# A recurrent decoder layer done by halves of its tokens, with the next layer's key parts on ScalarE

## The chip, the cores and the metric

The kernel runs on one core of a Trainium2 chip. Its metric is the device time of one execution in microseconds (us). Engines are named as the profile names them: PE is TensorE (PEld its weight loads), DVE is VectorE, ACT is ScalarE, POOL is GpSimd, SP is SyncE, whose queue issues nearly all transfers.

## The reference, cut to what matters

Four decoder layers run on 1024 tokens of 128 features; each has a mixing part ("attn"), a cross-attention over a context of 6404 rows ("xattn") and a feed-forward part ("ffn"), each with a layer norm ahead and a residual behind. The change is in the mixing part of layer 2, a gated recurrence with a small MLP. For its input `x` (the layer-normed tokens) it computes, cut to the core:

```python
h = rmsnorm(x, norm1_w)
gate = h @ W_gate.T                      # 192 channels
u = h @ W_in.T
u = causal_conv(u, conv_w) + conv_b      # 4 taps a channel
ig, rg = u @ rg_in_w.T + rg_in_b, u @ rg_gate_w.T + rg_gate_b
alpha = exp(-8 * softplus(forget_lambda) * sigmoid(rg))
xbeta = sqrt(1 - alpha * alpha + 1e-06) * sigmoid(ig) * u
hrec[t] = alpha[t] * hrec[t - 1] + xbeta[t]
x = x + (gelu(gate) * hrec) @ W_out.T
n2 = rmsnorm(x, norm2_w)
return x + (gelu(n2 @ mlp_gate_w.T) * (n2 @ mlp_up_w.T)) @ mlp_down_w.T
```

Behind it, the cross-attention of layer 2 takes queries from the tokens and keys from the context (`k = context @ Wk.T`).

## The kernel before

`build` (L1879) calls the twelve parts in order. Inside a part the statements are handed to a scheduler that sets the order of instructions on each engine and adds the semaphore waits, so an engine's order can differ from the order of the code; each engine takes its instructions strictly in its order. The tokens stay in SBUF as `x` (`x_tok` in the profile), token-major: 128 partitions by 8 tiles of 128 features. `xT` is the normed input with the features on the partitions and 1024 tokens along the row.

`l2_attn` (L1055) is the part that is changed. In order:

- L1079 to L1091 make the constants of `forget_lambda` (`sp`), tiny 96x2 instructions that each need the one before.
- L1094 `normalised` (L291: statistics, a square root on ACT, eight multiplications) writes `xn`; `rmsnormed` (L310) makes `r` from it: one square of 128x1024, one reduction, a square root on ACT, eight multiplications by tiles; `transposed` (L278) turns it into `xT` by PE in two halves of 512 tokens (`BANK` is 512), which DVE evicts with the factor `n1` (L289).
- L1103 to L1108: products of `xT` with `W_gate` (evicted by ACT with Gelu) and `W_in` (evicted by DVE into `up`), by cuts of 96 channels and halves of tokens. PE runs them through `hidden` (L338); the profile calls its line L343.
- L1111 to L1115: the convolution on DVE, per cut one L1112 and three L1114 over all 1024 tokens.
- L1119 to L1125: the two gates (`ig`, `al`), two products each, a sigmoid on ACT, and Exp on `al`.
- L1127 to L1135: `be = sqrt(1 - al*al)`, times `ig` on POOL (L1130), times `u` on DVE, then the scan (one instruction for each cut, along 1024 tokens, L1134) and the product with `gate`, all over 1024 tokens.
- `onto` (L1138) projects to the tokens and adds, both halves in one call; then the second norm and transposition, `x += xn` on POOL (L1153), the MLP (L1155 to L1160) and `onto` again.

Between these, `beside(n)` takes n steps of the generator `split_keys` (L1185), which prepares the next layer's keys: 13 chunks of up to 512 context rows. A chunk is one PE product (L1209), a copy to SBUF on DVE (`k`, L1212), and `split` (L1172): a cast to bf16 on DVE (L1178), the rest on POOL (L1179), a cast of the rest on DVE (L1180), a last subtraction on POOL (L1181), and six transfers of 128 KB by SP (L1183) into `kd2` in DRAM. `k` and `rest` have one buffer, the parts have three. The order of `beside` is 2, 2, 1, 2, 3 chunks; `_run(keys)` takes the last three. Layer 3's keys go through the same generator with a bias `bk`, and its queries and layer 2's through `split`.

`l2_xattn` (L1375) reads the key parts back (`kP`, L1397), makes its queries (L1404), projects the values (L1236) and then runs score products (L1339).

Of the kernel before, what the change touches and what calls it, by code (L numbers as in the profile page):

```python
# [10 lines left out]
F32 = mybir.dt.float32  # L11
# [4 lines left out]
ALU = mybir.AluOpType  # L16
# [195 lines left out]
class Decoder:  # L212
# [62 lines left out]
    def m(self, ps):  # L275
        return ps.tile([P, BANK], F32, tag="m", name="m")

    def transposed(self, ps, dst, src, scale=None):  # L278

        nc = self.nc  # L280
        for h in range(2):
            m = self.m(ps)
            for i in range(4):
                nc.tensor.transpose(m[:, i * P:(i + 1) * P], src[:, 4 * h + i, :], self.ident)  # L284
            o = dst[:, h * BANK:(h + 1) * BANK]
            if scale is None:
                self.copy(o, m)
            else:
                nc.vector.tensor_scalar(o, m, scale, None, ALU.mult)  # L289
# [17 lines left out]
        self.normalised(self.xn, self.x)  # L307
        self.transposed(ps, self.xT, self.xn)

    def rmsnormed(self, out, src, tmp):  # L310

        nc = self.nc
        rs = self.sm.tile([P, NT], F32, tag="rs", name="rms")
        nc.vector.tensor_tensor(tmp, src, src, ALU.mult)
        nc.vector.tensor_reduce(rs, tmp, AX.X, ALU.add)
        nc.scalar.activation(rs, rs, AF.Sqrt, bias=self.eps[:, 0:1], scale=1.0 / D)
        nc.vector.reciprocal(rs, rs)
        for t in range(NT):
            nc.vector.tensor_scalar(out[:, t, :], src[:, t, :], rs[:, t:t + 1], None, ALU.mult)

    def add_bias(self, b):

# [732 lines left out]
    def l2_attn(self):  # L1055
# [6 lines left out]
        with tc.tile_pool(name="h", bufs=1) as pool, tc.tile_pool(name="h_ps", bufs=2, space=PSUM) as ps0:  # L1062
# [7 lines left out]
            def beside(n):  # L1070
                for _ in range(n):
                    next(keys, None)

            def small(name):
                return pool.tile([96, 2], F32, tag=name, name=name)


            y, z, z2, sp = small("sp_y"), small("sp_z"), small("sp_z2"), small("sp")
            nc.vector.scalar_tensor_tensor(y, lam, -1.0, lam, ALU.mult, ALU.min)  # L1079
# [10 lines left out]
            nc.vector.scalar_tensor_tensor(sp, sp, 2.0, y, ALU.mult, ALU.add)  # L1090
            nc.vector.tensor_scalar(sp, sp, -8.0, None, ALU.mult)  # L1091

            beside(2)
            self.normalised(self.xn, self.x)  # L1094
            beside(2)
            tmp = pool.tile([P, NT, D], F32, tag="tmp", name="tmp")
            r = pool.tile([P, NT, D], F32, tag="r", name="r")
            self.rmsnormed(r, self.xn, tmp)
            self.transposed(ps, self.xT, r, n1)
            gate = pool.tile([96, 2, S], F32, tag="gate", name="gate")  # L1100
            up = pool.tile([96, 2, S + 3], F32, tag="up", name="up")
            nc.gpsimd.memset(up[:, :, 0:3], 0.0)
            for c in range(2):  # L1103
                cs = slice(96 * c, 96 * c + 96)
                for h, hs, m in self.hidden(ps, [wgate[:, cs]], [self.xT]):
                    nc.scalar.activation(gate[:, c, hs], m[:96, :], AF.Gelu)
                for h, hs, m in self.hidden(ps, [win[:, cs]], [self.xT]):
                    nc.vector.tensor_copy(up[:, c, 3 + h * BANK:3 + (h + 1) * BANK], m[:96, :])  # L1108
            beside(1)
            u = pool.tile([96, 2, S], F32, tag="u", name="u")  # L1110
            for c in range(2):  # L1111
                nc.vector.tensor_scalar(u[:, c, :], up[:, c, 0:S], cw[:, 4 * c:4 * c + 1], cb[:, c:c + 1], ALU.mult, ALU.add)  # L1112
                for k in range(1, 4):
                    nc.vector.scalar_tensor_tensor(u[:, c, :], up[:, c, k:k + S], cw[:, 4 * c + k:4 * c + k + 1], u[:, c, :],  # L1114
                                                   ALU.mult, ALU.add)  # L1115
            ig = pool.tile([96, 2, S], F32, tag="ig", name="ig")
            al = pool.tile([96, 2, S], F32, tag="al", name="al")
            be = pool.tile([96, 2, S], F32, tag="be", name="be")
            for c in range(2):  # L1119
                for o, wt, bias in ((ig, wri, bi), (al, wrg, bg)):  # L1120
                    for _, hs, m in self.hidden(ps, [wt[:, 192 * i + 96 * c:192 * i + 96 * c + 96] for i in range(2)],
                                                [u[:, i, :] for i in range(2)]):
                        nc.scalar.activation(o[:, c, hs], m[:96, :], AF.Sigmoid, bias=bias[:, c:c + 1])
            for c in range(2):
                nc.scalar.activation(al[:, c, :], al[:, c, :], AF.Exp, scale=sp[:, c:c + 1])  # L1125
            beside(2)
            nc.vector.tensor_tensor(be, al, al, ALU.mult)  # L1127
            nc.vector.tensor_scalar(be, be, -1.0, 1.0, ALU.mult, ALU.add)
            nc.scalar.activation(be, be, AF.Sqrt, bias=self.eps[:96, 1:2])
            nc.gpsimd.tensor_tensor(be, be, ig, ALU.mult)  # L1130
            nc.vector.tensor_tensor(be, be, u, ALU.mult)
            rec = pool.tile([96, 2, S], F32, tag="rec", name="rec")
            for c in range(2):
                nc.vector.tensor_tensor_scan(rec[:, c, :], al[:, c, :], be[:, c, :], 0.0, ALU.mult, ALU.add)  # L1134
            nc.vector.tensor_tensor(rec, rec, gate, ALU.mult)  # L1135
            beside(3)

            def onto(dst, src, wt):  # L1138

                for h in range(2):  # L1140
                    m = self.m(ps)
                    for i in range(4):
                        t = 4 * h + i
                        for c in range(2):
                            nc.tensor.matmul(m[:, i * P:(i + 1) * P], lhsT=src[:, c, t * P:(t + 1) * P],
                                             rhs=wt[:, c * P:(c + 1) * P], start=c == 0, stop=c == 1)
                    d = dst[:, 4 * h:4 * h + 4, :].rearrange("p t d -> p (t d)")
                    nc.vector.tensor_tensor(d, d, m, ALU.add)

            onto(self.xn, rec, wout)  # L1150
            self.rmsnormed(r, self.xn, tmp)
            self.transposed(ps, self.xT, r, n2)
            nc.gpsimd.tensor_tensor(self.x, self.x, self.xn, ALU.add)  # L1153
            _run(keys)
            for c in range(2):  # L1155
                cs = slice(96 * c, 96 * c + 96)
                for _, hs, m in self.hidden(ps, [wmg[:, cs]], [self.xT]):
                    nc.scalar.activation(gate[:, c, hs], m[:96, :], AF.Gelu)
                for _, hs, m in self.hidden(ps, [wmu[:, cs]], [self.xT]):
                    nc.vector.tensor_tensor(gate[:, c, hs], gate[:, c, hs], m[:96, :], ALU.mult)  # L1160
            onto(self.x, gate, wdown)

# [4 lines left out]

    KPART, QPART = (0, 1, 2, 0, 1, 0), (0, 0, 0, 1, 1, 2)  # L1170

    def split(self, pool, src, dst, which, a, b):  # L1172

        nc = self.nc
        n = b - a
        p = [pool.tile([P, BANK], BF16, tag=f"part{i}", name=f"part{i}", bufs=3) for i in range(3)]
        rest = pool.tile([P, BANK], F32, tag="rest", name="rest")
        nc.vector.tensor_copy(p[0][:, :n], src)  # L1178
        nc.gpsimd.tensor_tensor(rest[:, :n], src, p[0][:, :n], ALU.subtract)  # L1179
        nc.vector.tensor_copy(p[1][:, :n], rest[:, :n])  # L1180
        nc.gpsimd.tensor_tensor(p[2][:, :n], rest[:, :n], p[1][:, :n], ALU.subtract)  # L1181
        for i, k in enumerate(which):
            nc.sync.dma_start(out=dst[:, i, a:b], in_=p[k][:, :n])  # L1183

    def split_keys(self, ps, pool, w, kd, bk=None, mask=None):  # L1185
# [19 lines left out]
        for c in range((NK + BANK - 1) // BANK):  # L1205
            a, b = c * BANK, min((c + 1) * BANK, NK)
            n = b - a
            m = self.m(ps)
            nc.tensor.matmul(m[:, :n], lhsT=w, rhs=self.ctxT[:, a:b], start=True, stop=True)  # L1209
            k = pool.tile([P, BANK], F32, tag="k", name="k")  # L1210
            if bk is None:
                nc.vector.tensor_copy(k[:, :n], m[:, :n])  # L1212
            else:
                nc.vector.tensor_scalar(k[:, :n], m[:, :n], bk, None, ALU.add)
            self.split(pool, k[:, :n], kd, self.KPART, a, b)
            yield
            if mask is not None:
                row = pool.tile([1, BANK], F32, tag="row", name="row", bufs=1)
                self.mask_row(row[:, :n], rows, 4 * c, n)
                m = self.m(ps)  # L1220
                nc.tensor.matmul(m[:, :n], lhsT=first, rhs=row[:, :n], start=True, stop=True)  # L1221
                bar = pool.tile([P, BANK], BF16, tag="bar", name="bar")
                nc.vector.tensor_copy(bar[:, :n], m[:, :n])
                nc.sync.dma_start(out=kd[:, 6, a:b], in_=bar[:, :n])
                nc.sync.dma_start(out=kd[:, 7, a:b], in_=three[:, :n])
                yield
# [679 lines left out]
```

## Time and profile before

| what | us |
|---|---|
| median of 3 runs shown | 6175.1 |
| lowest and highest of them | 6174.22, 6192.93 |
| the profiled execution's own time | 6182.17 |
| its span | 6180.4 |
| from the last addition of layer 1 (3620.4) to the last addition of `l2_attn` (3732.8) | 112.4 |

Mean granted TensorE clock over the span: 0.944. A time such as 3620.4 is counted from the span's start. The table of stretches of time gives the busy time of every engine in each stretch with the number of instructions in brackets, then the granted clock as a share of full speed and the transfer engines' share. A timeline has start, length, engine, line, operation, output and inputs, shapes, count, and in square brackets how long the engine had been idle and whose result ended it. The mean length of an instruction holds the time in which it was held up after its start.

### The profile page before, as it was taken

Reading aid. Unit: us, or ns where it says so; the run is one execution under the profiler, and the core shown is the slowest. Engines: PE = TensorE matmul, PEld = TensorE weight load, DVE = VectorE, ACT = ScalarE, POOL = GpSimd, SP = SyncE. Lnnn points to the kernel's source line nnn. Section 1 sums busy time; section 2 is a strip of 40 time slices with the busy share of each in tenths; the row PEclk is TensorE's granted clock in tenths of the full one; section 3 lists DMA queues with packets and bytes.
Section 4 is the critical chain, followed back from the end, with each engine's and each line's share of the span. In section 5 each row is a group of like instructions: output and inputs, shape, how many; then the busy total and the mean of one; then the engine's idle time right before and its main releaser. Section 6 shows DMA issues by size and latency. Waiting matters only on the chain. (4 is left out here: it accounts for less than half of the span.)

```text
span 6180.4 us, 72184 instructions
## 1 busy us (share of the span) xinstructions
PE 5749.6 (93%) x29144; PEld 2078.1 (34%) x29144; DVE 3757.0 (61%) x4571; ACT 3096.5 (50%) x4041; POOL 2254.1 (36%) x1088
## 2 busy tenths in 40 slices
PE   5899999999999999999899968999989689999999
PEld 2333333333333434333476423111124311111126
DVE  6587777777777777776325552100014799999923
ACT  2434444444444444444211225899951167888872
POOL 2057767677777767678321541100001000000000
PEclk7899999999999999999979977999999689999999
DMA  3000000000000000000000013200022100000000
GB/s 113 4 1 1 1 1 1 1 1 1 1 1 1 1 1 1 1 17 18 33 1 14 0 58 87 88 11 7 1 83 80 54 1 22 1 22 1 1 6 29
DMA packets 65200, 117.97 MB, mean 19 GB/s; under 512 B 10475, under 2 KB 46673, under 8 KB 63201
## 3 DMA queue, kind: packets, MB, share of 16 engines
q1 hardware_dynamic: 64288, 110.08, 5.5%
q8 instruction: 228, 3.74, 0.3%
q10 hardware_dynamic: 576, 3.28, 0.1%
q14 instruction: 108, 0.88, 0.0%
HBM read 81.88 MB, written 31.42 MB: 18 GB/s over the span
## 5 line engine op out<-in xcount | busy, mean ns | idle before, releaser
L741 POOL TENSOR_TENSOR tot<-tot,p 128x1024 f32<-128x1024 f32 (+1 forms) x800 | 1889.8, 2362 | 584.5 <-ACT p L732 569.0
L732 ACT ACTIVATE p<-p,drop,keep 128x1024 f32<-128x1024 f32 (+1 forms) x816 | 1011.8, 1240 | 1321.7 <-DVE p L731 1260.0
L669 DVE TENSOR_REDUCE mx<-m 128x2 f32<-128x1024 f32 (+1 forms) x832 | 982.4, 1185 | 496.3 <-PE m L668 479.8
L1275 DVE TENSOR_REDUCE mx<-m 128x2 f32<-128x1024 f32 (+4 forms) x928 | 1027.1, 1159 | 93.5 <-PE m L265 82.2
L731 DVE TENSOR_TENSOR p<-s,every 128x1024 f32<-128x1024 f32 (+1 forms) x816 | 991.5, 1215 | 73.2 <-PE s L726 34.7
L1347 ACT ACTIVATE p<-s 128x512 f32<-128x512 f32 (+4 forms) x1620 | 819.7, 588 | 238.8 <-PE s L265 238.0
L668 PE MATMUL m<-kT,qT 64*128 64x512 f32 (+1 forms) x3328 | 888.6, 606 | 12.3 <-DVE mx L669 11.6
L1344 ACT ACTIVATE p<-s 128x1024 f32<-128x1024 f32 x918 | 843.9, 1185 | 31.5 <-PE s L1339 24.1
L726 PE MATMUL s<-qT,kT 64*128 64x512 f32 (+1 forms) x3264 | 837.7, 596 | 16.6 <-DVE p L731 15.4
L713 PE MATMUL acc<-p,v 128*64 128x512 f32 (+1 forms) x3264 | 809.4, 606 | 4.8 <-ACT p L732 3.8
L1318 PE MATMUL acc<-p,v 128*8 128x512 f32 (+2 forms) x3672 | 621.9, 597 | 0.0
L265 PE MATMUL m<-kP,qP 64*128 64x512 bf16 (+4 forms) x1856 | 371.5, 396 | 102.7 <-DVE mx L1275 57.0
L726 PEld LDWEIGHTS s<-qT,kT 64*128 64x128 f32 (+1 forms) x3264 | 321.7, 185 | 412.5 <-issue 342.1
L668 PEld LDWEIGHTS m<-kT,qT 64*128 64x128 f32 x3328 | 280.7, 185 | 504.1 <-DVE mx L669 371.4
L265 PE MATMUL acc<-p,v 128*9 128x512 f32 (+2 forms) x3240 | 422.2, 593 | 0.0
L265 PE MATMUL s<-qP,kP 64*128 64x512 bf16 (+4 forms) x1620 | 384.0, 387 | 8.9 <-ACT p L1347 6.2
L713 PEld LDWEIGHTS acc<-p,v 128*64 128x64 f32 (+1 forms) x3264 | 198.8, 136 | 550.9 <-issue 457.9
L1339 PE MATMUL s<-qP,kP 48*128 48x512 bf16 (+2 forms) x1836 | 281.0, 384 | 2.7 <-ACT p L1344 1.9
L271 DVE COPY oT<-acc 128x512 f32<-128x512 f32 x14 | 9.7, 690 | 404.4 <-PE acc L1318 395.7
L387 POOL MEMSET mpad<- 128x512 f32 x2 | 1.1, 529 | 641.2 <-PE m L1428 600.4
L265 PEld LDWEIGHTS <-qP 64*128 64x128 bf16 x1856 | 122.7, 96 | 319.6 <-issue 261.9
L265 PEld LDWEIGHTS <-kP 64*128 64x128 bf16 (+1 forms) x1620 | 83.7, 94 | 352.3 <-issue 347.4
(484 smaller groups left out, 4512.5 us busy)
## 6 DMA issues: line engine op xcount, KB each, us to landing
kd<-part SPq DMA_DIRECT2D x156, 128.0 KB, 1.9
wb<-expert_weights SPq DMA_DIRECT2D x30, 512.0 KB, 3.7
kP<-kd SPq DMA_DIRECT2D x24, 512.0 KB, 3.6
kP<-kd SPq DMA_DIRECT2D x48, 192.0 KB, 4.5
w_expert<-in_Y_w SPq DMA_DIRECT2D x8, 768.0 KB, 4.2
qd<-part SPq DMA_DIRECT2D x36, 128.0 KB, 1.8
qP<-qd SPq DMA_DIRECT2D x16, 256.0 KB, 6.2
ctxT<-in_ctxT ACTq DMA_DIRECT2D x4, 800.5 KB, 6.5
```

The source lines that it names most:

```text
L265: return self.tc.keep_in_program_order(self.nc.tensor.matmul(*a, **k))
L668: nc.tensor.matmul(m[:, j, :b - a], lhsT=qT[r, q0:q0 + P], rhs=kT[r, a:b], start=True, stop=True)
L669: tc.keep_in_program_order(nc.vector.tensor_reduce(mx[:, t, :, c:c + 1], m[:, :, :b - a], AX.X, ALU.max))
L713: nc.tensor.matmul(acc[64 * j:64 * j + 64, :], lhsT=v[:n, t, 64 * j:64 * j + 64], rhs=pr[:n, j, :], start=t == 0, stop=t == NKT - 1, tile_ ...
L726: nc.tensor.matmul(s[:n, j, :], lhsT=kT[r, t * P:t * P + n], rhs=qT[r, hs], start=True, stop=True)
L731: tc.keep_in_program_order(nc.vector.tensor_tensor(pr[:n], s[:n], every[:n], ALU.add))
L732: nc.scalar.activation(pr[:n], pr[:n], AF.Exp, bias=drop[:n, t:t + 1], scale=keep[:n, t:t + 1])
L741: nc.gpsimd.tensor_tensor(tot[:n], tot[:n], pr[:n], ALU.add)
L1275: nc.vector.tensor_reduce(mx[:, t, 2 * pair:2 * pair + 2, c:c + 1], m[:, :, :b - a], AX.X, ALU.max)
L1318: matmul(acc[32 * j:32 * j + v.shape[3], off:], lhsT=v[:n, t, 4 * g + j, :], rhs=ws[j][:n, :BANK - off], start=t == 0, stop=t == nkt - 1, ...
L1344: nc.scalar.activation(p2[:n], both[:n], func)
L1347: nc.scalar.activation(pp[j][:n, :w], ss[j][:n, :w], func)
```

## The change

`l2_attn` is rewritten by halves of the tokens; what follows it stands 14 or 15 lines further down.

- `rmsnormed` takes a half `h`: four tiles, its own `rs`. `transposed` takes a list of halves. Each half is normed and transposed by itself.
- The products with `W_in` come ahead of those with `W_gate` and are copied to `up` by ACT.
- The convolution, the gates, Exp, `al*al`, the square root, the products and the scan run on 512 tokens at a time. The scan of the second half starts from the last column of the first (`rec[:, c, BANK - 1:BANK]`). POOL multiplies `ig` with `u` (ahead of the square root) in place of `be` with `ig`.
- The gated result goes to `be`, `onto` does one half a call, and the second norm, the transposition and POOL's `x += xn` follow by halves, as does the MLP.
- The constants of `forget_lambda` stand in the code behind the convolution and the gates.
- Layer 2's key chunks: the copy out of PSUM and both casts go to ACT (`nc.scalar.copy`), where there is no bias; `beside` takes 3, 3, 4 chunks, `_run(keys)` three.

```diff
-    def rmsnormed(self, out, src, tmp):
+    def rmsnormed(self, out, src, tmp, h):
...
+        ts = slice(4 * h, 4 * h + 4)
+        rs = self.sm.tile([P, 4], F32, tag=f"rs{h}", name="rms")
+        nc.vector.tensor_tensor(tmp[:, ts, :], src[:, ts, :], src[:, ts, :], ALU.mult)
...
+            beside(3)
+            self.normalised(self.xn, self.x)
+            beside(3)
...
+            for h in range(2):
+                self.rmsnormed(r, self.xn, tmp, h)
+                self.transposed(ps, self.xT, r, n1, (h,))
...
+            for h, hs in enumerate(halves):
+                for c, cs in enumerate(cuts):
+                    nc.scalar.copy(up[:, c, 3 + h * BANK:3 + (h + 1) * BANK], product([win[:, cs]], [self.xT[:, hs]]))
+            for hs in halves:
+                for c, cs in enumerate(cuts):
+                    nc.scalar.activation(gate[:, c, hs], product([wgate[:, cs]], [self.xT[:, hs]]), AF.Gelu)
...
+            for h, hs in enumerate(halves):
+                for c in range(2):
+                    nc.vector.tensor_scalar(u[:, c, hs], up[:, c, hs], cw[:, 4 * c:4 * c + 1], cb[:, c:c + 1], ALU.mult, ALU.add)
+                    for k in range(1, 4):
+                        nc.vector.scalar_tensor_tensor(u[:, c, hs], up[:, c, k + h * BANK:k + (h + 1) * BANK],
+                                                       cw[:, 4 * c + k:4 * c + k + 1], u[:, c, hs], ALU.mult, ALU.add)
+                for o, wt, bias in ((al, wrg, bg), (ig, wri, bi)):
...
+                        nc.scalar.activation(o[:, c, hs], m, AF.Sigmoid, bias=bias[:, c:c + 1])
+                nc.gpsimd.tensor_tensor(ig[:, :, hs], ig[:, :, hs], u[:, :, hs], ALU.mult)
...
-            nc.scalar.activation(be, be, AF.Sqrt, bias=self.eps[:96, 1:2])
-            nc.gpsimd.tensor_tensor(be, be, ig, ALU.mult)
-            nc.vector.tensor_tensor(be, be, u, ALU.mult)
...
-                nc.vector.tensor_tensor_scan(rec[:, c, :], al[:, c, :], be[:, c, :], 0.0, ALU.mult, ALU.add)
-            nc.vector.tensor_tensor(rec, rec, gate, ALU.mult)
...
+            beside(4)
+            for hs in halves:
+                for c in range(2):
+                    nc.scalar.activation(al[:, c, hs], al[:, c, hs], AF.Exp, scale=sp[:, c:c + 1])
+                nc.vector.tensor_tensor(be[:, :, hs], al[:, :, hs], al[:, :, hs], ALU.mult)
+                nc.vector.tensor_scalar(be[:, :, hs], be[:, :, hs], -1.0, 1.0, ALU.mult, ALU.add)
+            for h, hs in enumerate(halves):
+                nc.scalar.activation(be[:, :, hs], be[:, :, hs], AF.Sqrt, bias=self.eps[:96, 1:2])
+                nc.vector.tensor_tensor(be[:, :, hs], be[:, :, hs], ig[:, :, hs], ALU.mult)
+                for c in range(2):
+                    nc.vector.tensor_tensor_scan(rec[:, c, hs], al[:, c, hs], be[:, c, hs],
+                                                 rec[:, c, BANK - 1:BANK] if h else 0.0, ALU.mult, ALU.add)
+                nc.vector.tensor_tensor(be[:, :, hs], rec[:, :, hs], gate[:, :, hs], ALU.mult)
...
+            for h in range(2):
+                onto(self.xn, be, wout, h)
+                self.rmsnormed(r, self.xn, tmp, h)
+                self.transposed(ps, self.xT, r, n2, (h,))
+                hs = slice(4 * h, 4 * h + 4)
+                nc.gpsimd.tensor_tensor(self.x[:, hs, :], self.x[:, hs, :], self.xn[:, hs, :], ALU.add)
             _run(keys)
...
-    def split(self, pool, src, dst, which, a, b):
+    def split(self, pool, src, dst, which, a, b, cast=None):
+        cast = cast or nc.vector.tensor_copy
...
-        nc.vector.tensor_copy(p[0][:, :n], src)
+        cast(p[0][:, :n], src)
...
-        nc.vector.tensor_copy(p[1][:, :n], rest[:, :n])
+        cast(p[1][:, :n], rest[:, :n])
...
-                nc.vector.tensor_copy(k[:, :n], m[:, :n])
+                nc.scalar.copy(k[:, :n], m[:, :n])
...
-            self.split(pool, k[:, :n], kd, self.KPART, a, b)
+            self.split(pool, k[:, :n], kd, self.KPART, a, b, nc.scalar.copy if bk is None else None)
```

## The prediction

> **What bounds the kernel now.** I read the profile's page first: PE is busy 93% of the span, so a change off PE can pay only where PE stands idle. The edited part is `l2_attn`, found by the lines of its additions: L336 at 3620.4, L1148 last at 3732.1 to 3732.8, hence 112.4 us, 1.8% of the span. The stretches of time, cut where the work changes hands, say who is busy in it:
>
> ```profile
> core 0: us, PE busy (x) PEld busy (x) DVE busy (x) ACT busy (x) POOL busy (x), PEclk, DMA share, GB/s
> 3620.40:3642.40 22.00, 7.08 (x17) 3.29 (x18) 21.63 (x60) 4.66 (x6) 9.58 (x9) 0.69 0.41 137
> 3642.40:3661.60 19.20, 16.28 (x30) 5.50 (x28) 13.68 (x16) 3.65 (x5) 3.71 (x2) 0.82 0.14 48
> 3661.60:3675.00 13.40, 13.16 (x31) 5.07 (x30) 2.23 (x5) 11.41 (x14) 1.79 (x2) 1.00 0.06 20
> 3675.00:3704.00 29.00, 0.00 (x0) 0.00 (x0) 24.10 (x17) 3.27 (x2) 20.82 (x10) 0.58 0.38 127
> ...
> 3732.80:3782.10 49.30, 33.14 (x116) 24.98 (x118) 16.68 (x39) 0.89 (x2) 4.61 (x4) 0.52 0.84 219
> 3782.10:4640.00 857.90, 836.81 (x5155) 171.43 (x5154) 72.67 (x161) 759.17 (x831) 29.97 (x29) 0.98 0.11 35
> ```
>
> The first four I call A, B, C, D; E, F, G are 3704.0 to 3711.7 (projection), to 3718.1 (norm) and to 3732.8 (MLP). In A DVE has no room left (21.63 of 22.00). In D PE does nothing for 29 us and ACT only 3.27: this is DVE and POOL work. DVE's own timeline shows what stands in it:
>
> ```profile
> 3675.72 2.28 DVE L1127 TENSOR_TENSOR be<-al 96x2048 f32<-96x2048 f32 x1
> 3679.04 0.43 DVE L1180 CAST part<-rest 128x512 bf16<-128x512 f32 x1 [1.05 <-POOL rest L1179]
> 3679.38 1.22 DVE L1128 TENSOR_SCALAR be<-be 96x2048 f32<-96x2048 f32 x1
> ...
> 3684.29 0.88 DVE L1178 CAST part<-k 128x512 bf16<-128x512 f32 x1
> 3686.50 4.70 DVE L1180 CAST part<-rest 128x512 bf16<-128x512 f32 x1 [1.33 <-POOL rest L1179]
> 3691.12 0.68 DVE L1212 COPY k<-m 128x512 f32<-128x512 f32 x1
> 3691.83 0.88 DVE L1178 CAST part<-k 128x512 bf16<-128x512 f32 x1
> 3692.63 2.28 DVE L1131 TENSOR_TENSOR be<-be,u 96x2048 f32<-96x2048 f32 x1
> 3695.95 0.43 DVE L1180 CAST part<-rest 128x512 bf16<-128x512 f32 x1 [1.05 <-POOL rest L1179]
> 3696.30 5.37 DVE L1134 TENSOR_TENSOR_SCAN rec<-al,be 96x1024 f32<-96x1024 f32 x2
> ```
>
> A cast of 0.43 takes 4.70 while POOL runs L1130 (4.49 from 3686.42): one waits for the other to end. The recurrence's four DVE steps (L1127, L1131, L1134, L1135) stand in one queue with the key chunks, whose casts wait for POOL. So D is the queue's length, not the recurrence's.
>
> **The change, stretch by stretch.** I laid the changed kernel's instructions out in the order in which its build puts them on each engine, each starting when its inputs are there, with lengths from rows of this profile. Halved shapes: a two-input DVE instruction of 2048 columns takes 2.28, of 1024 1.21 (L314, 128x1024), of 512 0.68 (L1046); L1114 of 1024 takes 1.28, so 0.74 for 512; L1112 0.81, so 0.54; the scan 2.28, so 1.21. On ACT, Exp of 1024 takes 1.15 and the square root of 2048 2.00, which makes 0.72 (512) and 1.15 (1024).
>
> *The key chunks.* DVE loses 13 copies (0.69) and 26 casts (0.43 free, up to 4.70 held up). On ACT the copy costs 0.59 (L273, PSUM to SBUF, 128x512). No row has ACT writing bf16; SBUF to SBUF in f32 ACT takes 0.63 (L439), the only row with bf16 on one side 0.81 (L593, read with two more operands). I take 0.63, the nearest, with 0.43 and 0.81 as ends: the casts have slack nearly everywhere and either end moves the sum by under 2. The second half's scan takes its start from a column; two column operands cost L1112 about 0.12 over L1128's rate, so 0 to 0.2 in all, taken as 0. The Trainium skill's page Perfetto Trace Analysis (Optimizing Scalar/DVE Operations) says that DVE is the faster one where it has a performance mode: the rows agree, 0.43 against 0.63, and were all of the 26 x 0.2 = 5 us on the path, the gain below would be 16. On ACT they stand in a queue that holds little of the recurrence. POOL's two subtractions a chunk (1.15 each) and SP's 78 transfers stay as they are.
>
> *A, 22.0 to 19.0.* Four chunks leave DVE: 4 x 0.60 (a copy's share of the queue) plus eight casts, 3.4, is 5.8. Given back: fixed costs of halves 0.6, the first norm's square root standing in ACT's queue behind a cast that waits for POOL (1.5), POOL in the way of the multiplications (0.7). Ends: gain 0 to 5.8, taken 3.0. The constants of `sp` gain nothing by their place: the scheduler puts them ahead of the norm's multiplications as before. They are 15 steps of 0.19, done 5.0 after the addition, where the norm's square root is ready 4.6 after it.
>
> *B, 19.2 to 13.5.* Before, the convolution starts at 3648.15, 5.75 behind the end of A: PE makes two gate products first and each takes 1.71 at the granted clock of 0.5. Now the products with `W_in` come first and start with the first half of `xT`, 2.9 before the second is there; 1.9 for one product and 0.59 for ACT's copy, and the convolution starts about when A ends. Its own work stays: 4 x (0.54 + 3 x 0.74) = 11.0 plus three POOL subtractions in its way (0.8 each), 13.5, against 13.4 before with the copies in between. Gain 5.7.
>
> *C, 13.4 to 12.5.* PE's 16 gate products (0.86 at full clock) start with the first half of `u`, 4.5 ahead of the end of the convolution, and end 8.6 behind it; then a sigmoid 0.68, a switch of table 1.28, Exp, a key copy and Exp. From the first sigmoid to the square root ACT loads seven tables where it loaded five; the two added (1.28 each) lie beside PE's products. The Trainium skill, page ScalarE: Activation LUTs (What ACT_TABLE_LOAD costs), adds a drain of 1.38 us to every switch, 2.66 in all; that would lengthen the six behind the first sigmoid by 8.3 and leave a gain of 12.7. The trace doesn't show it: a sigmoid ends at 3672.50, the load starts at 3672.52, and Exp 0.01 behind it.
>
> *D, 29.0 to 18.3.* Work left on DVE behind the last Exp: nine two-input instructions of 1.21 or scans of the same length, and one of 0.68: 11.6. POOL still has four chunks here, eight subtractions, and holds up DVE as L1134 shows (scans of 2.28 and 3.17 with POOL at 3.06): seven of them by 0.9 is 6.3, and 0.4 of waits. Ends: none held up, 12.0; all ten behind a whole 1.15, 23.5. What goes is the waiting of DVE's queue for POOL, and POOL's hold-ups are what is late next. The multiplication by `ig` (4.49 on POOL, in the path) is gone from it: POOL does `ig*u` in C. Gain 10.7, between 5.5 and 17.
>
> *E, F, G: 7.7, 5.9, 14.5.* Halves should overlap here, and mostly don't. The first half's 16 projection instructions (3.4 of 6.9) run beside the second scan, but PE's order puts the transposition of the first half ahead of the second half's projection, so that waits for the first half's norm on DVE (3.0): E stays 7.7. F gains 0.5 by the smaller square and reduction. In G, PE has two to three key products and eight MLP products either way (0.86 each, 1.71 before the clock rises); gain 0.2.
>
> Sum: 3.0 + 5.7 + 0.9 + 10.7 + 0 + 0.5 + 0.2 = **21.0 us**, `l2_attn` in 91.4.
>
> *Behind it.* The order on every engine is the same up to `l2_attn` and after it, but for a 1 MB load of weights that SP issues 75 transfers later, hundreds of us ahead of its use in the next part. Up to the first score product 49.3 us go by, set by PE and its one eviction buffer (L1236 and L1240, 13 times 2.86); the key parts read back land 33 us before. So nothing takes the gain back.
>
> Profiled execution: 6182.2 - 21.0 = 6161.2. It stands 7.1 above the median of the runs shown; the median less 21.0 is **6154.1 us**.
>
> **The rivals.**
> - *ACT's queue binds.* ACT now has casts that wait for POOL, ahead of square roots and sigmoids of the path. I have counted three: ahead of the norm's first square root, of Gelu, and of the second half's square root. If five more each cost what a held-up POOL subtraction costs over a free one (3.07 - 1.15 = 1.9), 9.6 go: gain 11.4, 6163.7, within 0.3%. For: POOL is held up in D now. Against: ACT sits idle 25 of D's 29 us.
> - *A switch of table costs twice its load* where it stands between dependent steps: six of 1.28 on the path are 7.7, gain 13.3, 6161.8. Against: the 0.02 above. The drain in the Trainium skill's page ScalarE: Activation LUTs (What ACT_TABLE_LOAD costs) would be such a cost.
> - *ACT's cast is dear, and the kernel slower.* ACT is busy 28.2 in `l2_attn` now. Added: copies 7.7, `up` 2.4, two loads 2.6, halves 1.0, and 26 casts of c. In order, it also waits for POOL's first subtraction once a chunk, 13 x 1.45 = 18.9. That is 60.8 + 26c: level at c = 2.0, and at c = 2.7 it is 131, 18.6 over, 6193.7. For: no row shows this cast. Against: 0.63 and 0.81.
> - *It doesn't do what it says.* True of the constants, as shown; nothing else.
>
> **How the numbers follow.** 0.3% of 6175 is 18.5 us, about what a measurement of this kernel can tell from no change. Forecast 0.82, ACT's queue 0.12, switches 0.02, dear cast 0.04. The forecast's own ends come from A and D: gains of 12.8 and 30.1 with both at one end, of which I take 15 to 28. The gain passes 18.5 in about three quarters of the forecast's share: faster 0.62; the rest of it, the queue and the switches are within 0.3%: 0.34; slower 0.04. Range: 6147 (median less 28) to 6166 (the profiled execution less 16, since the runs shown spread that way, and past both of the middle rivals).
>
> **What would show it.** Right: `l2_attn` at about 91 us; D under 20 us, with DVE free of key lines; the convolution starting within 1 us of the second half of `xT`; an ACT cast near 0.6. Wrong: ACT casts over 1 us; idle times of ACT in D ended by POOL's `rest` with a square root behind them; gaps of over 1 us at table loads; POOL subtractions of 2 to 3 us throughout D; or a longer stretch between the last addition and the first score product, which would mean that the keys' transfers are in the path.

## The result, and the profile after

The changed kernel takes 6159.1 us (median of 7 runs, 6154.84 to 6161.26), the kernel before on the same chip 6177.93 (7 runs): 18.8 us less, ratio 0.9962 with a 95% interval of 0.9951 to 0.9974. The prediction was 6154.1 in 6147 to 6166, faster by over 0.3%. By the ratio the gain is 0.38%; its interval, 0.26% to 0.49%, leaves open whether it is above 0.3%. The profiled execution took 6155.63; its span is 6153.8, 26.6 less than that of before. The last addition of layer 1 now starts at 3618.2 and the last addition of `l2_attn` ends at 3710.8, so the part takes 92.6 where it took 112.4.

The stretches of time of the changed kernel, A to G in the first seven rows, then the way to the first score product and the scores behind it (columns as in the table of before):

```profile
3618.20:3637.90 19.70, 10.81 (x24) 4.59 (x24) 16.89 (x52) 11.62 (x21) 10.33 (x9) 0.78 0.40 134
3637.90:3651.30 13.40, 11.94 (x27) 4.24 (x26) 13.33 (x17) 10.66 (x17) 5.16 (x4) 0.93 0.46 157
3651.30:3663.80 12.50, 12.12 (x29) 4.56 (x27) 1.99 (x3) 12.37 (x17) 4.69 (x2) 1.00 0.00 0
3663.80:3682.50 18.70, 3.75 (x16) 3.48 (x16) 18.21 (x11) 9.64 (x15) 12.97 (x8) 0.58 0.42 144
3682.50:3690.80 8.30, 4.50 (x20) 4.24 (x20) 4.48 (x11) 0.30 (x1) 1.77 (x1) 0.50 0.17 57
3690.80:3696.80 6.00, 3.48 (x8) 1.86 (x9) 3.13 (x9) 1.50 (x3) 1.77 (x1) 0.50 0.01 3
3696.80:3710.80 14.00, 12.68 (x52) 6.82 (x50) 5.24 (x16) 7.96 (x13) 5.97 (x6) 0.97 0.43 142
3710.80:3757.40 46.60, 31.28 (x110) 23.84 (x110) 15.94 (x38) 0.89 (x2) 4.61 (x4) 0.51 0.91 212
3757.40:4615.00 857.60, 837.70 (x5156) 172.43 (x5156) 72.25 (x161) 759.70 (x831) 30.01 (x29) 0.98 0.11 36
```

DVE is down from 21.63 to 16.89 in A, and ACT up from 4.66 to 11.62: the key lines have changed engines. D is 18.7 where it was 29.0, and DVE is still busy through nearly all of it (18.21). DVE's timeline shows with what:

```profile
3663.93 1.22 DVE L1141 TENSOR_TENSOR be<-al 96x1024 f32<-96x1024 f32 x1 [4.33 <-ACT al L1140]
3665.18 1.53 DVE L1142 TENSOR_SCALAR be<-be 96x1024 f32<-96x1024 f32 x1
3666.97 1.22 DVE L1145 TENSOR_TENSOR be<-be,ig 96x1024 f32<-96x1024 f32 x1 [0.26 <-ACT be L1144]
3668.22 4.08 DVE L1147 TENSOR_TENSOR_SCAN rec<-al,be 96x512 f32<-96x512 f32 x2
3672.23 2.11 DVE L1145 TENSOR_TENSOR be<-be,ig 96x1024 f32<-96x1024 f32 x1
3674.26 2.17 DVE L1150 TENSOR_TENSOR be<-rec,gate 96x1024 f32<-96x1024 f32 x1
3676.35 4.19 DVE L1147 TENSOR_TENSOR_SCAN rec<-al,rec,be 96x512 f32<-96x512 f32 x2
3680.58 1.99 DVE L1150 TENSOR_TENSOR be<-rec,gate 96x1024 f32<-96x1024 f32 x1
```

No key line is left, only the recurrence in halves; but a product over 512 tokens that takes 1.22 when free takes 2.0 to 2.2, and a scan 2.06 to 2.17. POOL's subtractions stand beside them. ACT's timeline in the same stretch shows whether its queue binds:

```profile
3667.76 1.15 ACT L1144 ACTIVATE be<-be,eps 96x1024 f32<-96x1024 f32 x1
3668.81 0.60 ACT L1193 CAST part<-k 128x512 bf16<-128x512 f32 x1
3671.26 0.62 ACT L1195 CAST part<-rest 128x512 bf16<-128x512 f32 x1 [1.85 <-POOL rest L1194]
```

ACT waits for POOL here, but behind the last square root, where nothing of the recurrence stands in its queue any more. For the first square root, which stands behind a key cast (0.61) and its table load, DVE waits 0.26 (in the timeline above). The cast takes 0.60 to 0.62.

### The profile page after: what moved, and what is told of

Read it like the earlier page. It is cut to its first block, busy times and chain, and to the rows that moved or that the text cites. A ratio compares the mean times of both kernels' runs of the same rounds, so it can differ in the third digit from the quotient of the medians.

```text
span 6153.8 us, 72228 instructions
## 1 busy us (share of the span) xinstructions
PE 5746.4 (93%) x29144; PEld 2076.6 (34%) x29144; DVE 3740.3 (61%) x4548; ACT 3122.0 (51%) x4091; POOL 2251.7 (37%) x1090
## 5 line engine op out<-in xcount | busy, mean ns | idle before, releaser
L669 PE MATMUL m<-kT,qT 64*128 64x512 f32 (+1 forms) x3328 | 889.5, 607 | 12.5 <-DVE mx L670 11.5
```

What stands on the lines that cost most here:

```text
L669: nc.tensor.matmul(m[:, j, :b - a], lhsT=qT[r, q0:q0 + P], rhs=kT[r, a:b], start=True, stop=True)
```

## The experiments

Three figures are used below: the length of the part (from the last addition of layer 1 to the last of `l2_attn`), the time from the same start to the first score product, and to the 401st exponential of the scores on ACT, some 440 us behind the part. For before they are 112.4, 161.6 and 556.1, for the changed kernel 92.6, 139.2 and 534.4.

**Which half of the change does it: e1, the key lines back on DVE.**

```diff
-                nc.scalar.copy(k[:, :n], m[:, :n])
+                nc.vector.tensor_copy(k[:, :n], m[:, :n])
...
-            self.split(pool, k[:, :n], kd, self.KPART, a, b, nc.scalar.copy if bk is None else None)
+            self.split(pool, k[:, :n], kd, self.KPART, a, b, None)
```

> The halves stay, the key copies and casts go back to DVE. The part took 112.4 us before and 92.6 after. If the gain is wholly DVE's queue being free of key work, it goes back to about 112. If it is wholly the halves, it stays near 92.6. My theory is that both count and add up: DVE has 13 copies and 26 casts more, part of them held up by POOL, in the stretches of the norm and of the scan, so about 101.5, and the median between those of the two kernels.

6169.94 (median of 10 runs; before 6179.11), ratio 0.9984 [0.9974, 0.9993]. Part 102.5, first score product 149.0. Its stretches A and D:

```profile
3615.00:3641.70 26.70, 10.41 (x24) 4.62 (x24) 26.22 (x66) 4.25 (x7) 14.09 (x13) 0.70 0.50 167
...
3665.40:3687.80 22.40, 3.75 (x16) 3.49 (x16) 18.91 (x21) 3.65 (x4) 12.61 (x8) 0.60 0.42 141
```

With the halves alone A is longer than before (26.7 against 22.0), because six chunks now stand there in place of four and DVE has no room (26.22 of 26.70); B is shorter still (10.4): no chunk is left for it, and POOL does nothing there.

**The other half: e2, the kernel before with the key lines on ACT.**

```diff
-                nc.vector.tensor_copy(k[:, :n], m[:, :n])
+                nc.scalar.copy(k[:, :n], m[:, :n])
...
-        nc.vector.tensor_copy(p[0][:, :n], src)
+        cast(p[0][:, :n], src)
...
-        nc.vector.tensor_copy(p[1][:, :n], rest[:, :n])
+        cast(p[1][:, :n], rest[:, :n])
```

> The kernel before, with the key copies and casts on ACT and nothing else changed. By DVE's queue alone the part falls to about 92; by the halves alone it stays at 112. My theory: about 105, since 4.5 us of POOL's product with ig and whole-length steps one behind another stay in the path; the multiplication on POOL then stands ahead of or behind key subtractions as before.

6172.82 (median of 10 runs), ratio 0.9991 [0.9981, 1.0]. Part 105.8, first score product 154.5. A falls by 4.0, to 18.0, but D only by 1.2, to 27.8, though no key line is left on DVE there. DVE's timeline of D is complete in five lines:

```profile
3671.17 2.29 DVE L1127 TENSOR_TENSOR be<-al 96x2048 f32<-96x2048 f32 x1 [13.88 <-ACT al L1125]
3673.49 2.06 DVE L1128 TENSOR_SCALAR be<-be 96x2048 f32<-96x2048 f32 x1
3686.36 3.22 DVE L1131 TENSOR_TENSOR be<-be,u 96x2048 f32<-96x2048 f32 x1 [10.81 <-POOL be L1130]
3689.62 6.22 DVE L1134 TENSOR_TENSOR_SCAN rec<-al,be 96x1024 f32<-96x1024 f32 x2
3695.87 3.06 DVE L1135 TENSOR_TENSOR rec<-rec,gate 96x2048 f32<-96x2048 f32 x1
```

DVE stands idle for 10.81 and waits for the product with `ig` on POOL. ACT's timeline shows the other thing in the way: its square root, whose input is there at 3675.5, stands behind a cast that waits for POOL.

```profile
3677.82 0.62 ACT L1180 CAST part<-rest 128x512 bf16<-128x512 f32 x1 [1.57 <-POOL rest L1179]
3678.46 1.28 ACT L1129 ACT_TABLE_LOAD   x1
3679.76 2.00 ACT L1129 ACTIVATE be<-be,eps 96x2048 f32<-96x2048 f32 x1
```

So one half of the change gives 6.6, the other 9.9, both 19.8: 3.3 more than the sum. Of this, 2.5 stands in D, where the halves take off 6.6 (22.4), the move 1.2 (27.8) and both 10.3 (18.7): each alone leaves there what the other removes. The rest is what remains of differences both ways in A, B, C, E and G, which were not taken apart.

**Does POOL hold up the recurrence: e3, no key chunk beside it.**

```diff
-            beside(4)
+            beside(0)
```

> The changed kernel with beside(4) made beside(0): no key chunk is handed out at the scan, the last seven run at the MLP. If POOL's subtractions hold up DVE at the scan, the stretch from the last Exp to the gated result falls from 18.7 to about 12.5 and each scan to 1.2; if the recurrence's own steps set it, it stays above 17. What is saved should come back: seven chunks of about 2.8 behind the second norm outlast the MLP, so the part falls by 2 to 3 only and the first value projection behind it comes no earlier than now.

6158.9 (one run). DVE's timeline of D:

```profile
3663.08 2.36 DVE L1145 TENSOR_TENSOR be<-be,ig 96x1024 f32<-96x1024 f32 x2 [0.58 <-ACT be L1144]
3665.36 2.33 DVE L1147 TENSOR_TENSOR_SCAN rec<-al,be 96x512 f32<-96x512 f32 x2
3667.61 1.25 DVE L1147 TENSOR_TENSOR_SCAN rec<-al,rec,be 96x512 f32<-96x512 f32 x1
3668.79 1.19 DVE L1150 TENSOR_TENSOR be<-rec,gate 96x1024 f32<-96x1024 f32 x1
```

The same instructions take 1.2 each without POOL beside them, and D is 11.9: the hold-ups are 6.8 of the changed kernel's 18.7. But the part is only 2.0 shorter (90.6): E takes 1.1 more, G, where the four chunks now stand in a row with the last three, 4.0 more, and the first score product (142.2) and the 401st exponential (537.5) come 3.0 later than in the changed kernel. Work that is taken from here has to go somewhere.

**PE's order in E: e4, both halves projected first.** In the changed kernel PE does the transposition of the first half ahead of the projection of the second:

```profile
3679.69 0.63 PE L1158 MATMUL m<-w_H,be 96*128 96x128 f32 x2
3685.63 0.45 PE L284 MATMUL m<-ident,r 128*128 128x128 f32 x1 [5.31 <-DVE r L320]
3685.87 0.63 PE L1158 MATMUL m<-w_H,be 96*128 96x128 f32 x2
```

```diff
+            _ = [onto(self.xn, be, wout, h) for h in range(2)]
             for h in range(2):
-                onto(self.xn, be, wout, h)
                 self.rmsnormed(r, self.xn, tmp, h)
```

> The changed kernel with both halves' projections handed out ahead of the second norms. If PE's order (the first half's transposition ahead of the second half's projection) is what keeps the halves from overlapping there, the stretch from the gated result to the second half's addition falls from 8.3 to about 4.5, of which the norms behind it take back about half: the part ends 1.5 to 2 earlier. If PE or DVE work itself set it, nothing changes.

6161.23 (one run). E is 4.6 where it was 8.3, F 8.1 where it was 6.0; part 91.0, first score product 137.5. The order on PE does cost E 3.7, of which the norm takes 2.1 back: DVE's norms of the two halves then follow each other. The 1.6 that is left does not last: the 401st exponential comes at 535.4, no sooner than in the changed kernel (534.4, and 535.2 in e5).

**Is the time of one execution to be trusted: e5, the changed kernel again.**

> The changed kernel once more, beside the next one on the same chip. My theory (the gain of 19.8 us lies in the part, and what is ahead of it and behind it differs from execution to execution by some 4 us): part 92.6 within 0.5, stretches as before within 0.3, first score product 139.2 behind the last addition of layer 1, and a time 16 to 23 us under the kernel before. Rival (the 26.6 us between the two profiled executions are the change's, and come again): 25 us or more under it.

6163.26 (median of 6 runs, 6141.87 to 6165.7), ratio 0.9964 [0.9951, 0.9977] to 6180.37 of before. Part 92.6, every stretch as in the first profile to 0.1, first score product 139.2, 401st exponential 535.2. Its profiled execution took 6146.19, 9.4 less than the first: its part began 13.3 sooner, at 3604.9 rather than 3618.2, and what follows the first score product took 4.0 longer. In the ten executions profiled here, whose instructions ahead of the part are the same, it begins between 3604.9 and 3623.2; the spread is as large as the gain. So the 26.6 us between the two first spans are 2.2 from ahead of the part, 22.4 up to the first score product, and 2.0 from behind it; only the middle is the change's.

**Both together, and the chunks where DVE waits anyway: e6.**

```diff
-            beside(4)
+            beside(0)
...
+            _ = [onto(self.xn, be, wout, h) for h in range(2)] + [beside(4)]
             for h in range(2):
-                onto(self.xn, be, wout, h)
```

> The changed kernel with two edits together: both halves are projected before the first is normed, and the four key chunks that stood beside the recurrence are put right behind the two projections. My theory (POOL's subtractions hold up DVE in D, and the first half's transposition ahead of the second half's projection holds up PE in E; the key chunks cost little in E and F, where DVE waits for PE and ACT): D falls from 18.7 to 11.5 to 13, E from 8.3 to 4 to 5.5, F and G together grow by no more than 5; the part is 84 to 88, and the first score product comes 5 to 8 us sooner than in the changed kernel, so that the time is 4 to 8 us under it. Rival (the chunks cost the same wherever they stand, as the look with all of them at the end suggested: saved in D, given back behind it): the part is 88 to 91, the first score product within 2 us of the look that only projects first (137.5), and the time is 2 us or less under the changed kernel.

6151.61 (median of 5 runs, 6150.3 to 6154.13), ratio 0.9951 [0.9940, 0.9963] to before. That is 11.7 under the median of e5 on the same chip, where 4 to 8 had been expected; but two of e5's six executions (6141.87 and 6146.19) lie below all of these, and the intervals overlap, so that the times alone do not part the two. The traces do. Stretches D to G:

```profile
3664.60:3676.50 11.90, 2.24 (x10) 2.27 (x11) 11.17 (x10) 3.52 (x4) 0.00 (x0) 0.54 0.00 0
3676.50:3681.00 4.50, 4.50 (x26) 4.09 (x25) 2.71 (x5) 0.30 (x1) 1.77 (x1) 0.71 0.00 0
3681.00:3689.70 8.70, 5.81 (x19) 2.72 (x18) 7.25 (x15) 4.80 (x9) 6.82 (x6) 1.00 0.40 136
3689.70:3703.80 14.10, 11.85 (x51) 6.49 (x49) 5.17 (x15) 9.88 (x18) 9.47 (x9) 1.00 0.66 222
```

POOL is idle in D now. F and G are 2.8 longer than in the changed kernel (22.8 against 20.0), of which 2.1 came with e4 (22.1): the chunks themselves cost 0.7 there. The part is 84.4, the first score product at 133.1 and the 401st exponential at 528.4, 6.0 to 6.8 ahead of the changed kernel. The chunks do not cost the same wherever they stand.

**Where B's gain comes from: e7, the products with `W_gate` first, as before.**

```diff
-            for h, hs in enumerate(halves):
-                for c, cs in enumerate(cuts):
-                    nc.scalar.copy(up[:, c, 3 + h * BANK:3 + (h + 1) * BANK], product([win[:, cs]], [self.xT[:, hs]]))
-            for hs in halves:
-                for c, cs in enumerate(cuts):
+            for c, cs in enumerate(cuts):
+                for hs in halves:
                     nc.scalar.activation(gate[:, c, hs], product([wgate[:, cs]], [self.xT[:, hs]]), AF.Gelu)
+                for h, hs in enumerate(halves):
+                    nc.scalar.copy(up[:, c, 3 + h * BANK:3 + (h + 1) * BANK], product([win[:, cs]], [self.xT[:, hs]]))
```

> The changed kernel with the products in the order of the kernel before: by cuts, W_gate's two halves with Gelu, then W_in's two halves with ACT's copy. My theory (B's gain of 5.8 is the place of the products with W_in: the convolution starts when the first of them is copied): the first product with W_in now comes behind two with W_gate, of which the second needs the second half of xT, so the convolution starts 2 to 3.5 behind the end of A rather than with it, and the second cut's first half, the seventh product, comes later still; B is 15.5 to 18 rather than 13.4, the part 2 to 4.5 longer, A, D, E unchanged within 0.3. Rival (B is set by DVE's own work in halves, and the early start is given back as waits further on): B and C together are within 0.7 of 25.9.

6169.07 (one run). DVE's timeline where A ends:

```profile
3638.78 0.75 DVE L289 TENSOR_SCALAR xT<-m,w_H 128x512 f32<-128x512 f32 x1 [1.91 <-PE m L284]
3644.10 0.54 DVE L1110 TENSOR_SCALAR u<-up,w_H 96x512 f32<-96x512 f32 x1 [4.57 <-ACT up L1102]
```

DVE waits 4.57 for the first copy of `up`, so that the convolution starts 4.6 behind the end of A (2 to 3.5 had been expected): PE starts the second product with `W_gate` at 3639.68, when the second half of `xT` is there, and this product, the first with `W_in` and ACT's copy take 4.3 together. B is 17.7 rather than 13.4; C and D grow by 0.8 and 0.4, and the part is 5.2 longer (97.8), 0.7 past the expected range. The early place of the products with `W_in` is worth all of that.

**The constants, really behind: e8.** `lam` is read through a sum with zero times `u`.

```diff
+            lam2 = small("lam2")
+            nc.vector.scalar_tensor_tensor(lam2, u[:, 0, 0:2], 0.0, lam, ALU.mult, ALU.add)
-            nc.vector.scalar_tensor_tensor(y, lam, -1.0, lam, ALU.mult, ALU.min)
+            nc.vector.scalar_tensor_tensor(y, lam2, -1.0, lam2, ALU.mult, ALU.min)
...
-            nc.vector.tensor_scalar(y, lam, 0.0, None, ALU.max)
+            nc.vector.tensor_scalar(y, lam2, 0.0, None, ALU.max)
```

> The changed kernel with the constants of forget_lambda really behind the convolution: lam is read through a sum with zero times two columns of u, so that no scheduler can put the 15 steps and their Exp ahead of the norm. My prediction's view (the place of the constants gains nothing, since the norm's square root is not ready before them): A stays 19.7 within 0.4. Rival, from the trace of the changed kernel (the Exp of the constants brings a table load of 1.28 and stands ahead of the key copy and the square root in ACT's queue): the square root is ready 1.3 to 1.6 sooner and A falls by as much, to 18.1 to 18.5. For both: behind the convolution the Exp of the constants takes two more switches between the sigmoids (1.28 each, or 2.66 each if a switch cost twice its load) and 15 steps of 0.19 ahead of the first Exp on al, so that C grows by 2 to 5 and the part does not get shorter.

6157.42 (one run). A is 19.5, 0.2 less, so the rival's 1.3 to 1.6 is not there. ACT's key copy ahead of the square root waits for PE there, and the square root starts only 0.25 sooner behind the last addition (3.86 for 4.11). B is 1.0 and C 2.3 longer, the part 95.4. ACT's timeline shows the two added switches:

```profile
3643.18 1.26 ACT L1118 ACTIVATE al<-m,w_H 96x512 f32<-96x512 f32 x2
3644.45 1.28 ACT L1126 ACT_TABLE_LOAD   x1
3646.16 0.20 ACT L1126 ACTIVATE sp_y<-sp_y 96x2 f32<-96x2 f32 x1 [0.42 <-DVE sp_y L1125]
3646.38 1.28 ACT L1118 ACT_TABLE_LOAD   x1
3647.67 1.26 ACT L1118 ACTIVATE ig<-m,w_H 96x512 f32<-96x512 f32 x2
```

A switch starts 0.01 to 0.02 behind the end of the instruction ahead of it and the next starts 0.01 behind it: 1.28 in all, not twice that.

## Why the prediction was right, and where it was not

| stretch | before | forecast | after |
|---|---|---|---|
| A norm, transposition | 22.0 | 19.0 | 19.7 |
| B products, convolution | 19.2 | 13.5 | 13.4 |
| C gates, Exp | 13.4 | 12.5 | 12.5 |
| D recurrence | 29.0 | 18.3 | 18.7 |
| E projection | 7.7 | 7.7 | 8.3 |
| F second norm | 6.4 | 5.9 | 6.0 |
| G MLP | 14.7 | 14.5 | 14.0 |
| sum | 112.4 | 91.4 | 92.6 |

- *The size.* The part gained 19.8 for a forecast 21.0. The forecast lies 5.0 below the result: 2.8 of that because the kernel before measured 6177.9 beside the changed one and not 6175.1, 2.2 because the medians differ by 18.8. Whether these 2.2 hold the part's own 1.2 or only the spread between executions can't be told from the times.
- *A.* Right in direction, 0.7 short. Moving the key lines alone took 4.0 off the 22.0 (e2); the halves alone added 4.7, with two chunks more in A (e1); both together leave 2.3. The 1.5 that the sum gave back for a square root behind a cast that waits for POOL did not come: the square root of the statistics has only a key copy (0.56) ahead of it, and that of the first half in `rmsnormed` starts 0.03 behind its input, at 3629.91. What the sum did not have is a wait at the end of A:

```profile
3637.19 0.75 DVE L289 TENSOR_SCALAR xT<-m,w_H 128x512 f32<-128x512 f32 x1 [1.91 <-PE m L284]
3637.86 0.53 DVE L1111 TENSOR_SCALAR u<-up,w_H 96x512 f32<-96x512 f32 x1
```

  DVE stands idle for 1.91: the last tile of `r` is there at 3635.29, but PE does the first product with `W_in` (from 3634.95) ahead of that tile's transposition (3636.73). That A came out near 19.0 is in part luck, then: one term was missing and another too many. With the keys on ACT and no halves A is 18.0 (e2); whether this wait is the 1.7 between was not tried. The constants cost nothing by their place, as the prediction had it: 0.2 in e8, and dearer when they stand behind.
- *B.* Right, and for the reason given: the convolution starts at 3637.86 (the second line above), as A ends, and 4.6 behind its end when the products with `W_in` come second (e7).
- *C.* Right. The switches lie beside PE's products, and a switch between two instructions that are ready costs no more than its load. The Trainium skill, page ScalarE: Activation LUTs (What ACT_TABLE_LOAD costs), has the load of 1283 ns as measured here and adds a drain of about 1380 ns to every switch; in the changed kernel's trace 13 of the 33 loads stand within 0.03 us of the instruction on either side and show no such drain (the others stand beside a wait, where it can't be told), and the part gained 19.8 where 12.7 would have been left with it.
- *D.* The sum was right: nine steps and one of 0.68, 11.6 when free (e3: 11.9 for the whole stretch), and hold-ups of 6.3 (6.8 measured; eight of the ten instructions are held up, by 0.8 to 1.0 each, where seven by 0.9 were counted). The Trainium skill, page SBUF — State Buffer (Who interferes with whom), says that a DVE instruction with two SBUF inputs contends with a GpSimd instruction that reads SBUF; the products here agree (1.99 to 2.17 for 1.22), and the scans, which it does not name, behave alike (2.06 to 2.17 for 1.2). So does L1142, with one input from SBUF (1.53 for 0.69). What failed is the sentence on the kernel before, **"So D is the queue's length, not the recurrence's"**. In e2 DVE's queue is empty of key lines and D is still 27.8. Of this an estimated 20.4 is the recurrence's own chain, its steps at their free lengths one behind another: on DVE 2.28 and 1.22, on ACT 1.28 for the load and 2.00, on POOL 4.49 for the product with `ig`, on DVE again 2.28, 4.56 for two scans and 2.28. Nearly all the rest is the key work, met on the other engines: for 2.9 the square root stands behind casts in ACT's queue, and POOL's subtractions hold up DVE's steps by 4.3. So emptying DVE's queue alone could bring D down to this chain at best, and brought 1.2, since part of the wait moved to another queue. The halves and the moved product shorten the chain itself, to 11.9 when nothing holds it up (e3).
- *E.* PE's order was read rightly, but its term of 0 was -0.6. e4 shows 3.7 of E to be that order.
- *Behind it.* **"The order on every engine is the same up to `l2_attn` and after it"** failed, to the good. PE's timeline has the last value product behind the first score products now, where the kernel before has it ahead of them:

```profile
3757.39 0.61 PE L1354 MATMUL s<-qP,kP 48*128 48x512 bf16 x2
3758.24 1.43 PE L1251 MATMUL m<-w_E,ctxT 128*128 128x128 f32 x6 [0.24 <-DVE v L1255]
3759.61 0.61 PE L1354 MATMUL s<-qP,kP 48*128 48x512 bf16 x4
```

The way from the part to the first score product is 46.6 for 49.2, so the gain there is 22.4. The length goes with the order: 46.5 in e1, e4, e5, e7 and e8, which have the changed kernel's, 48.7 to 51.7 in e2, e3 and e6, which have that of before. At the 401st exponential the gain is 21.7 (20.9 in e5), so that 1 to 2 of the 2.6 stay. The keys' transfers were not in the path, as said.

- *The rivals.* ACT's queue does not bind in the changed kernel: the second square root starts 1.05 behind its input, and ACT's waits of 1.85 to 2.37 come after it. It was no idle thought, though: in e2 the square root starts 4.2 behind its input, 1.28 of it the load. A cast takes 0.60 to 0.62 where 0.63 was taken, so nothing is left of the dear cast.

## What to carry to other kernels

A queue that is full is not yet the bound: before pricing what leaves it, follow the chain that would remain with the queue empty, over the other engines too, as e2 did for D, and ask in whose queue the moved work stands then. Side work has to stand where the engine it disturbs is waiting for something else; the same four chunks cost 6.8 beside the scans and 0.7 beside the second norm and the MLP (e6 against e4). When the gain is as small as the drift between executions, compare from a landmark ahead of the change to one behind it, in each trace by itself.

## What the runs showed of the hardware that was not expected

- The stretches of the part repeat to 0.1 us from one execution to another (e5), while its start moves by up to 18.4 us with the same instructions ahead of it. About half of that is there early: in the ten executions the 401st DVE instruction starts between 362.6 and 371.7. TensorE's granted clock goes with it: its mean over the first 300 us is 0.83 in e5, which is there first, 0.77 to 0.78 in the five that are there behind 370, and 0.79 to 0.81 in the other four. Whether the clock is the cause, and what moves it, was not tried.
- POOL's subtraction and DVE's instructions hold each other up both ways: 1.2 becomes 2.0 to 2.2 on DVE (e3 against the changed kernel), and POOL's, 1.15 when free, stretch too (the changed kernel's in D take 1.30 to 2.02). A second input is not needed for it: a multiplication of 128x128 by a column, 0.28 when free, takes 1.23 in A beside a subtraction that starts with it (3630.86).
